# Attention plus top-1 experts in one kernel: the split of the row maxima moved ahead of the pair's accumulating transfer in GpSimd's order

## The chip, the core and the metric

One core of a Trainium2 chip runs the whole program. Its engines are TensorE (PE in the profile; PEld are its weight loads), VectorE (DVE), ScalarE (ACT), GpSimd (POOL) and SyncE (SP), which only issues DMAs here. Each engine works through its own list of instructions in order, and engines wait for one another and for DMAs by semaphores. The core has 16 DMA engines. What SP issues goes to them through one queue (q1 in the profile), what GpSimd issues through another (q0). The metric is the device time of one execution in microseconds (us), less is better; the time of a kernel is the median of several runs.

## What is computed

Four sequences of 2048 tokens with 512 features pass through a layer norm, a multi-head attention and a layer of eight experts with a capacity of 100 tokens each. Both results are added to the input.

```
xn = layernorm(x)                               # x: 4 x 2048 x 512, float32
q, k, v = split(xn @ w_qkv); 16 heads of 32     # q and k filtered by a 32 x 32 matrix
attn = softmax(q @ k.T / sqrt(32))              # 2048 x 2048 for each head and sequence
out = x + (attn @ v) @ w_out + b_out + experts(xn)
```

Most of the work is the attention: 64 pairs of a sequence and a head, each with a 2048 x 2048 table of scores, its exponentials and its product with v.

## The kernel before

**Groups, blocks and windows.** The main loop takes groups k = 0 to 15, each one sequence with four heads (128 features). A group has four blocks n of 512 queries; I number the 64 blocks 0 to 63, so that block 4k + n is the block n of group k. A block has eight windows w of two key tiles j (`even` and `odd`, 128 keys each), 512 windows in all. The inner loop stands at lines 905 to 957.

**One window.** For each of its two key tiles and each half u of the heads, TensorE does three things: `shift` (lines 614 to 622) starts a PSUM bank with minus the row's maximum, by a matmul of ones with the tile `negm`; `max_matmuls` makes scores of a later block, which VectorE reduces to row maxima (`part`); `scores` adds q times k to the bank. ScalarE takes the exponential into the tile `even` or `odd` (128 x 2048 float32, 1 MB). One tile later `products` multiplies the tile with v, and VectorE adds that to `num`.

**The pair and the sums.** The softmax's denominator needs the sum of the exponential tiles. One window after the two tiles were made, `pair` (line 892) lets a DMA that GpSimd issues add `odd` to `even` in place, 1 MB with accumulation. Another window later `add_to` (line 895) lets GpSimd add the tile of the window before, in two instructions. The tile `even` has five buffers and `odd` has three, so a buffer of `odd` comes round after three windows and is free once the pair's transfer has landed.

**The maxima.** The maxima of a block are ready two windows ahead of the block. In its window 6 (counting in the block before the one that needs them) `max_close` (line 489) turns them by a matmul and ScalarE copies them to `row[:, 0]` and `rest`. In window 7 `max_split` (line 501) cuts them into three bfloat16 rows of falling size: four small GpSimd instructions, and three SP DMAs of 4 KB each into `negm`. The first of these DMAs needs ScalarE's copy alone, the second and third need GpSimd's. The first matmul of the next block, in `shift`, reads all three rows.

**The end of a block.** `close_steps` (line 649) is spread over the next ten windows: the sums go through DRAM to be inverted and come back as `factor`; in window 7 GpSimd multiplies `num` and `factor` to `ot` (`divide`, line 684); in the window after it TensorE multiplies `ot` with the output weights (`project`, from `result`, line 688).

**Orders.** Every engine keeps the order of the program (`InOrder`, line 71), SP's DMAs in the main loop too. At the start of a window GpSimd gets, in this order, the pair's transfer, the split (in window 7 alone), and the add; then come the steps of `agenda`, a list by window. Two of these matter here: `load_qkv_weights` (line 395, placed at line 861) issues a load of 768 KB (`wg`) on SP in window 6 of a group's last block, and in some groups `load` of 1 MB of x (`xs`) stands beside it (line 875). Projections of the next group are spread over the windows of a group, but for its last one.

Of the kernel before, what the change touches and what calls it, by code (L numbers as in the profile page):

```python
# [101 lines left out]
def attention_and_top1_experts(ctx: ExitStack, tc: tile.TileContext, a: dict, out: bass.AP):  # L102
# [14 lines left out]
    def bank():  # L117

        return array[:, next(turns), :]
# [36 lines left out]
    def chunk(name):  # L156
        tag, bufs = ("y", 1) if name == "y" else ("xs", None)
        return chunks.tile([P, TQ, DM], F32, tag=tag, name=name, bufs=bufs)

    def probs(odd):  # L160

        name = "odd" if odd else "even"
        return probs_pool.tile([P, 2, 2, QB], F32, tag=name, name=name, bufs=3 if odd else 5)
# [296 lines left out]
    def max_matmuls(item, half):  # L460
        k, n, m, t, u = item
        for h in range(2):
            at = DH * (2 * u + h)
            on.tensor.matmul(
                array[:, half[h], :],
                lhsT=qs[k, n][at : at + DH, t * P : (t + 1) * P],
                rhs=ks[k][at : at + DH, m * QB : (m + 1) * QB],
                start=True,
                stop=True,
            )  # L470

    def max_reduce(item, half):
        k, n, m, t, u = item
        if (k, n) not in parts:
            parts[k, n] = small.tile([P, HG, TQ, NQ], F32, name="part", bufs=2)
        for heads, scored in joined(*half):
            part = parts[k, n][:, 2 * u : 2 * u + 2, t, m]
            on.vector.reduce_max(part[:, heads], scored, axis=AX.X)
        if (m, t, u) == (NQ - 1, TQ - 1, 0):
            full_blocks.append((k, n))  # L480
# [3 lines left out]
    def max_negate(k, n):  # L484
        negs[k, n] = small.tile([P, HG * TQ], F32, name="neg")
        part = parts.pop((k, n)).rearrange("p h t m -> p (h t) m")
        on.vector.tensor_reduce(negs[k, n], part, AX.X, ALU.max, negate=True)

    def max_close(k, n):

        pn = bank()[0 : HG * TQ, 0:P]
        on.tensor.matmul(pn, lhsT=negs.pop((k, n)), rhs=ident, start=True, stop=True)
        rest = small.tile([HG * TQ, P], F32, name="rest")
        row = small.tile([HG * TQ, 3, P], BF16, name="row", bufs=2)
        on.scalar.copy(row[:, 0, :], pn)
        on.scalar.copy(rest, pn)
        closed[k, n] = rest, row
# [3 lines left out]
    def max_split(k, n):  # L501

        rest, row = closed.pop((k, n))
        for i in (1, 2):
            on.gpsimd.tensor_tensor(rest, rest, row[:, i - 1, :], ALU.subtract)
            on.gpsimd.tensor_copy(row[:, i, :], rest)
        negms[k, n] = qkv.tile([P, QB], BF16, tag="negm", name="negm", bufs=3)
        for i in range(3):
            on.sync.dma_start(out=negms[k, n][i::DH, :], in_=row[:, i, :])
# [93 lines left out]
    def scores(k, n, j, u, half):  # L603
        for h in range(2):
            at = DH * (2 * u + h)
            on.tensor.matmul(
                half[h],
                lhsT=ks[k][at : at + DH, j * P : (j + 1) * P],
                rhs=qs[k, n][at : at + DH, :],
                start=False,  # L610
                stop=True,
            )

    def shift(k, n, u, half):
        for h in range(2):
            at = DH * (2 * u + h)
            on.tensor.matmul(
                half[h],
                lhsT=ones_b[at : at + 3, :],
                rhs=negms[k, n][at : at + 3, :],  # L620
                start=True,
                stop=False,
            )
# [6 lines left out]
    def products(k, n, j, tile, num):  # L630
        po = bank()
        four_heads(po, lambda at: vs[k][:, j, at], tile, start=True, stop=True)
        if j == 0:
            on.scalar.copy(num, po)
        else:
            on.vector.tensor_tensor(num, num, po, ALU.add)
# [172 lines left out]
    def at(window, step, *args):  # L809
        agenda[window].append(lambda: step(*args))  # L810
# [81 lines left out]
    def pair(first, second):  # L892
        on.gpsimd.dma_start(out=first, in_=second, accum_op=ALU.add)

    def add_to(tile, sum_before, engine):
        for u in range(2):
            engine.tensor_tensor(tile[:, u], tile[:, u], sum_before[:, u], ALU.add)

    pairs, adds, full, splits = {}, {}, {}, {}
    left = None  # L900
    window = 0
    maxima = stream[MAX_AHEAD:]
    for k in range(B * NG):
        plan(k)
        for n in range(NQ):
            num = work.tile([P, QB], F32, tag="num", name="num")
            tiles = {}
            for w in range(NW):
                even, odd = w * WIN, w * WIN + 1
                if window in pairs:  # L910
                    pair(*pairs.pop(window))
                if window in splits:
                    max_split(*splits.pop(window))
                if window in adds:
                    add_to(*adds.pop(window))
                here = agenda[window]
                cut = (len(here) + 1) // 2
                for j in (even, odd):
                    tiles[j] = probs(j == odd)
                    for u in range(2):  # L920
                        half = bank(), bank()

                        mate = maxima.pop(0) if maxima else None
                        shift(k, n, u, half)
                        if mate:
                            mh = next(turns), next(turns)
                            max_matmuls(mate, mh)
                        scores(k, n, j, u, half)
                        for h in range(2):
                            on.scalar.activation(tiles[j][:, u, h, :], half[h], AF.Exp, scale=SCALE)  # L930
                        if mate:
                            max_reduce(mate, mh)
                    while full_blocks:
                        filled = full_blocks.pop(0)
                        max_negate(*filled)
                        full[window + 1] = filled
                    if left:
                        products(*left)
                    left = k, n, j, tiles[j], num
                    if j == even and window in full:  # L940
                        splits[window + 1] = full.pop(window)
                        max_close(*splits[window + 1])
                    for step in here[:cut] if j == even else here[cut:]:
                        step()
                last = (k, n) == (B * NG - 1, NQ - 1)
                if not last or w < NW - 2:
                    pairs[window + 1] = tiles[even], tiles[odd]
                    if 0 < w:

                        due, engine = (2, on.gpsimd) if maxima else (3, on.vector)  # L950
                        adds[window + due] = tiles[even], tiles[even - WIN], engine
                if last and w == NW - 2:
                    y = chunk("xs")
                    on.sync.dma_start(out=y, in_=o[B - 1, n])
                window += 1
            if not last:
                for after, *step in close_steps(k, n, num, tiles[NT - WIN]):
                    at(window + after, *step)
# [41 lines left out]
```

## Time and profile before

| what | value |
|---|---|
| time, median of 3 runs (lowest to highest) | 4525.47 us (4524.64 to 4526.17) |
| the profiled execution: time, span | 4519.14 us, 4517.2 us |
| TensorE busy | 4390.0 us, 97% of the span |
| GpSimd busy | 2919.2 us, 65% |
| VectorE busy, ScalarE busy | 3134.8 us, 2596.8 us |
| granted TensorE clock, mean | 0.987 |
| q0, the transfers that GpSimd issues | 605.83 MB, 68.9% of the 16 DMA engines' span |
| q1, the transfers that SP issues | 93.89 MB, 6.7% |
| pair's transfers | 510 of 1024 KB, landing a median of 8.1 us after the issue |
| GpSimd's TENSOR_TENSOR on `rest`, CAST to `row` | 128 each, 417 ns and 287 ns |
| GpSimd's `even` adds | 876, 2517 ns each |

The span runs from the first instruction to the last. Busy time of TensorE is from records in which a matmul's end is modelled, so a share of 97% says that it is nearly always at work, not that it is at its peak. A row of the waits names the engine and the tile that waited, what it waited for, the sum in us, the number of times and the longest. A row of the timeline gives a start, a length, the instruction, how many of them were merged, and in brackets how long the engine had been idle before it and for what. A row of the stretches (windows of the profile, not of the kernel) gives a stretch, its length, the busy time of each engine, then the granted TensorE clock, the busy share of the DMA engines (it can pass 1 in a short stretch, since a packet counts where it starts) and the GB/s moved.

### The profile page before, as it was taken

Reading aid. Unit: us, or ns where it says so; the run is one execution under the profiler, and the core shown is the slowest. Engines: PE = TensorE matmul, PEld = TensorE weight load, DVE = VectorE, ACT = ScalarE, POOL = GpSimd, SP = SyncE. Lnnn points to the kernel's source line nnn. Section 1 sums busy time; section 2 is a strip of 40 time slices with the busy share of each in tenths; the row PEclk is TensorE's granted clock in tenths of the full one; section 3 lists DMA queues with packets and bytes.
Section 4 is the critical chain, followed back from the end, with each engine's and each line's share of the span. In section 5 each row is a group of like instructions: output and inputs, shape, how many; then the busy total and the mean of one; then the engine's idle time right before and its main releaser. Section 6 shows DMA issues by size and latency. Waiting matters only on the chain. (4 is left out here: it accounts for less than half of the span.)

```text
span 4517.2 us, 106256 instructions
## 1 busy us (share of the span) xinstructions
PE 4390.0 (97%) x44398; PEld 1883.0 (42%) x44398; DVE 3134.8 (69%) x3642; ACT 2596.8 (57%) x4988; POOL 2919.2 (65%) x1993
## 2 busy tenths in 40 slices
PE   8999999999999999999999999999999999999998
PEld 4343433434434343444444434343443434434432
DVE  6667667766676777776666766677667765777776
ACT  3455555575555555557555555556655555555555
POOL 0677666765766666775676656667567665776673
PEclk9999999999999999999999999999999999999999
DMA  4677778886777777897677777789767866787778
GB/s 107 157 165 156 152 144 163 196 196 129 144 153 149 145 156 152 167 215 168 131 147 149 159 140 142 156 177 208 160 130 159 167 141 127 149 169 157 149 157 176
DMA packets 191546, 707.03 MB, mean 157 GB/s; under 512 B 47374, under 2 KB 52656, under 8 KB 125784
## 3 DMA queue, kind: packets, MB, share of 16 engines
q0 software_dynamic: 110432, 605.83, 68.9%
q1 hardware_dynamic: 79456, 93.89, 6.7%
q8 instruction: 347, 5.69, 0.5%
q14 instruction: 135, 1.11, 0.1%
q10 hardware_dynamic: 1176, 0.52, 0.0%
HBM read 76.03 MB, written 89.98 MB: 37 GB/s over the span
## 5 line engine op out<-in xcount | busy, mean ns | idle before, releaser
L82 DVE TENSOR_REDUCE part<-array 128x2 f32<-128x1024 f32 (+1 forms) x2313 | 2434.8, 1097 | 1251.7 <-PE array L82 1239.6
L82 PE MATMUL array<-k,q 32*128 32x512 f32 x8192 | 2242.4, 626 | 4.6 <-issue 2.2
L82 POOL TENSOR_TENSOR even<-even 128x1024 f32<-128x1024 f32 x876 | 2118.2, 2517 | 183.0 <-DMA even<-odd 181.8
L82 PE MATMUL array<-q,k 32*128 32x512 f32 x8192 | 2068.7, 598 | 0.8 <-issue 0.8
L82 ACT ACTIVATE even<-array 128x512 f32<-128x512 f32 x2048 | 1066.3, 601 | 540.9 <-PE array L82 536.7
L82 ACT ACTIVATE odd<-array 128x512 f32<-128x512 f32 x2048 | 1060.1, 602 | 429.0 <-issue 221.4
L82 POOL DMA_DIRECT2D even<-odd x510 | 442.0, 867 | 1227.6 <-ACT odd L82 1032.7
L82 PEld LDWEIGHTS array<-k,q 32*128 32x128 f32 x8192 | 811.3, 185 | 165.6 <-DVE num L82 68.4
L82 PE MATMUL array<-negm,ones_b 3*128 3x512 bf16 x4096 | 799.1, 384 | 78.7 <-DMA negm<-row 70.5
L82 PEld LDWEIGHTS array<-q,k 32*128 32x128 f32 x8192 | 755.3, 187 | 16.5 <-issue 6.8
L82 DVE TENSOR_TENSOR num<-num,array 128x512 f32<-128x512 f32 x960 | 651.2, 678 | 50.5 <-PE array L82 31.2
L82 PEld LDWEIGHTS <-ones_b 3*128 3x128 bf16 x4096 | 203.4, 92 | 968.7 <-issue 805.5
L82 PE MATMUL array<-even,v 128*32 128x512 f32 x4096 | 549.6, 607 | 14.4 <-ACT odd L82 14.4
L82 PE MATMUL array<-odd,v 128*32 128x512 f32 x4096 | 555.3, 613 | 4.7 <-ACT even L82 4.5
L82 PE MATMUL array<-xnT,wg 128*32 128x512 f32 x4096 | 465.5, 595 | 1.3 <-ACT xnT L82 0.7
L82 PE MATMUL array<-wo,ot 128*32 128x512 f32 x2048 | 259.3, 596 | 1.7 <-POOL ot L82 1.7
L82 PEld LDWEIGHTS array<-xnT,wg 128*32 128x32 f32 x4096 | 132.7, 111 | 307.2 <-issue 271.1
L82 PEld LDWEIGHTS array<-odd,v 128*32 128x32 f32 x4096 | 81.9, 109 | 405.6 <-ACT even L82 397.2
L82 PEld LDWEIGHTS array<-even,v 128*32 128x32 f32 x4096 | 81.1, 108 | 406.4 <-ACT odd L82 393.5
L82 PEld LDWEIGHTS array<-wg,xnT 128*32 128x32 f32 x8192 | 226.2, 110 | 41.4 <-issue 23.8
L82 PE MATMUL array<-wg,xnT 128*32 128x128 f32 x8192 | 235.7, 273 | 1.9 <-issue 1.9
L82 ACT COPY y<-array 128x512 f32<-128x512 f32 x252 | 147.7, 586 | 138.3 <-PE array L82 137.7
(127 smaller groups left out, 1354.5 us busy)
## 6 DMA issues: line engine op xcount, KB each, us to landing
even<-odd POOLq DMA_DIRECT2D x510, 1024.0 KB, 8.1
out_dram<-y POOLq DMA_DIRECT2D x63, 1024.0 KB, 12.1
xs<-in_L_attn_x_dram SPq DMA_DIRECT2D x30, 1024.0 KB
out_dram<-xs SPq DMA_DIRECT2D x16, 1024.0 KB
factor<-inverse SPq DMA_DIRECT2D x248, 64.0 KB
wg<-wd SPq DMA_DIRECT2D x15, 768.0 KB
wo<-in_L_attn_w_out_dram SPq DMA_DIRECT2D x16, 256.0 KB
negm<-row SPq DMA_DIRECT2D x192, 4.0 KB
```

Of the source, the lines that this page charges most:

```text
L82: done = act(*args, **kwargs)
```

## The change

In the inner loop the call of `max_split` moves from behind `pair` to ahead of it. Nothing else is altered: the same instructions and DMAs run, with the same tiles and buffers.

```
@@ -907,10 +907,10 @@
             for w in range(NW):
                 even, odd = w * WIN, w * WIN + 1
+                if window in splits:
+                    max_split(*splits.pop(window))
                 if window in pairs:
                     pair(*pairs.pop(window))
-                if window in splits:
-                    max_split(*splits.pop(window))
                 if window in adds:
                     add_to(*adds.pop(window))
                 here = agenda[window]
```

```
def max_split(k, n):
    rest, row = closed.pop((k, n))
    for i in (1, 2):
        on.gpsimd.tensor_tensor(rest, rest, row[:, i - 1, :], ALU.subtract)
        on.gpsimd.tensor_copy(row[:, i, :], rest)
    negms[k, n] = qkv.tile([P, QB], BF16, tag="negm", name="negm", bufs=3)
    for i in range(3):
        on.sync.dma_start(out=negms[k, n][i::DH, :], in_=row[:, i, :])

def pair(first, second):
    on.gpsimd.dma_start(out=first, in_=second, accum_op=ALU.add)
```

It touches 63 of the windows: window 7 of every block but the last, ahead of blocks 1 to 63. The split of block 0 stands ahead of the main loop and stays. On GpSimd the split's four instructions come ahead of the pair's issue. Among SP's instructions nothing changes places, since the pair's transfer is issued by GpSimd.

## The prediction

> **What bounds the kernel now.** TensorE is busy for 97% of the span, so I read the waits first, for what stops it.
>
> ```profile
> POOL even L82 <- ACT odd L82: 1032.7, 307, 12.1
> ...
> PE array L82 <- DMA negm<-row: 70.5, 22, 7.0
> ```
>
> TensorE's longest sum of idle time is 70.5 us, in 22 waits for the rows of the maxima. GpSimd waits 1032.7 us for ScalarE's `odd` tile, which is what the pair's issue needs, and the split is queued behind that issue. The timeline of GpSimd, SP and TensorE ahead of block 60 shows how the 22 come about:
>
> ```profile
> 4251.36 4.68 POOL L82 TENSOR_TENSOR even<-even 128x1024 f32<-128x1024 f32 x2 [1.46 <-DMA even<-odd]
> 4255.97 0.85 POOL L82 DMA_DIRECT2D even<-odd  x1
> 4256.57 0.42 POOL L82 TENSOR_TENSOR rest<-rest,row 16x128 f32<-16x128 f32 x1
> ...
> 4257.89 0.28 POOL L82 CAST row<-rest 16x128 bf16<-16x128 f32 x1
> 4258.14 4.65 POOL L82 TENSOR_TENSOR even<-even 128x1024 f32<-128x1024 f32 x2
> 4262.76 1.25 POOL L82 TENSOR_TENSOR ot<-num,factor 128x512 f32<-128x512 f32 x1
> ```
>
> ```profile
> 4257.35 0.54 SPq L82 DMA_DIRECT2D negm<-row  x1
> ...
> 4258.19 1.03 SPq L82 DMA_DIRECT2D negm<-row  x1
> ```
>
> ```profile
> 4263.77 0.61 PE L82 MATMUL array<-negm,ones_b 3*128 3x512 bf16 x2 [4.13 <-DMA negm<-row]
> ```
>
> The split begins 0.60 after the pair's issue and lasts 1.60 us (4256.57 to 4258.17); SP issues the last row 0.03 later. That row has 4 KB, but TensorE gets it only 5.6 us later. The stretches of the same time (length, five engines, granted clock, DMA share, GB/s) say why:
>
> ```profile
> 4256.50:4257.50 1.00, 1.00 (x12) 0.63 (x13) 0.95 (x2) 0.20 (x1) 0.85 (x4) 1.00 0.56 115
> ...
> 4261.50:4262.50 1.00, 0.00 (x0) 0.00 (x0) 0.00 (x0) 0.00 (x0) 1.00 (x1) 1.00 0.69 134
> 4262.50:4263.50 1.00, 0.00 (x0) 0.00 (x0) 0.00 (x0) 0.00 (x0) 1.00 (x2) 0.52 0.05 13
> 4263.50:4264.50 1.00, 0.73 (x6) 0.76 (x10) 0.00 (x0) 0.00 (x0) 1.00 (x2) 0.50 0.00 0
> 4264.50:4269.00 4.50, 4.50 (x26) 1.69 (x23) 2.39 (x2) 2.07 (x4) 4.50 (x3) 0.50 0.94 189
> ```
>
> The pair's megabyte moves until about 4262.2; the packet records have the rows' packets at 4262.4 to 4262.6, behind all of it. And TensorE's clock, which fell to half in the stall, stays there till 4269.
>
> **A rule against this change.** The Trainium skill ("DMA: Bandwidth & Descriptors", section on queues, rings and completion order) says that a DMA engine takes turns between its queues packet by packet. Then the pair would hardly hold back 4 KB, and the change would give only the earlier start: in the 22 places the split would begin 22 us earlier in sum (0.60 each, and 8.8 us of pair waits), so at most 22 us. The row decides: in block 60 the rows waited out a whole transfer.
>
> **The race to the queue.** In the new order the split begins when GpSimd's add and ScalarE's copy to `rest` are both over. In block 60 that is 4256.0 (the copy was done at 4250.6). It ends at 4257.6; the last row is issued at 4257.65, the pair at 4257.6. Who reaches the DMA engines first? Ahead of block 9 a row was issued on idle queues at 715.77, and stretches of 0.1 us show its packets from here:
>
> ```profile
> 716.80:716.90 0.10, 0.10 (x5) 0.07 (x1) 0.10 (x1) 0.10 (x1) 0.00 (x0) 1.00 0.00 0
> 716.90:717.00 0.10, 0.10 (x6) 0.00 (x0) 0.10 (x1) 0.10 (x1) 0.00 (x0) 1.00 0.10 23
> ```
>
> That is 1.18 us after its issue; its semaphore was complete at 717.4, after 1.65. The pair's issue at 4255.97 has its first large packet 1.43 later. So the last row is at the engines at 4258.83 and the pair at 4259.03: the row wins by 0.2 us and lands at 4259.3. TensorE is free for it at 4259.64 (4263.77 less 4.13). The stall is gone.
>
> **The stalls, block by block.** I did the same for all 22: new start, 1.60, 1.65, against the time at which TensorE came.
> - In 17 the row lands in time: 46.7 us.
> - Ahead of blocks 12, 28 and 36 SP has the `wg` load (in the first two also 1 MB of `xs`) in its queue ahead of the rows. There the first row, which the change doesn't touch, landed only at 931.0, 2031.4 and 2589.1, and the others can only follow it. Of 3.54, 3.60 and 4.64 us some 3.1, 3.1 and 2.5 stay: 3.0 us saved.
> - Ahead of blocks 61 and 63 GpSimd's add ends too late: of 4.97 and 7.04 some 1.0 and 3.1 stay: 7.9 us saved.
>
> Sum 57.6 us.
>
> **The clock.** After 16 of the stalls the q and k matmuls take 1.06 instead of 0.59 us for 2.3 to 4.2 us, 63.0 us together; half of that is lost, 31.5. It stays in blocks 12, 28, 36 and 63 (7.5), so 24.0 are saved. A check: the first windows of blocks 4, 32 and 48, after stalls too short for it, take 11.43 us; those of 8, 16, 20, 24, 36, 40 and 56 take 15.2 us more in sum, where half of their slow stretches is 13.5. The skill's page "TensorE: Matmul & The Clock Gate" (Part 1) has the half clock after an idle window of about 3.4 us. By that, ten stalls cost 1.7 each, and 10 us would be saved. But the records show half clock after stalls of 2.27, 2.35 and 2.52 us too; I take 24.0.
>
> **What is late next: `ot`.** In the window after the stall TensorE reads `ot` 3.02 us after its first matmul. GpSimd's `ot` doesn't come earlier where the pair's issue followed the add without a gap (split and issue only change places), and up to 1.6 us earlier elsewhere. TensorE now gets there first ahead of ten blocks (4, 16, 24, 32, 44, 48, 56, 60, 61, 62), by 0.8, 0.8, 0.3, 0.7, 0.6, 0.8, 3.4, 1.5, 1.7 and 0.8: a new wait of 11.4 us, and some 1.6 of half clock after the longest. Cost 13.0.
>
> **What I put at nothing.** The split's 1.60 us now stand ahead of the pair's issue. In some 40 of the 63 windows GpSimd had a gap there and it costs the transfer little; in the others the transfer starts up to 1.6 us later. Queued behind it are an add one window on, and `odd`'s buffer two windows on, some 11 us after the issue even in group 15, against 7 to 8 for the transfer. GpSimd idles 1227.6 us before 510 pair issues, 2.4 us a window, which takes up the add. Without that cover it would be at most 63 x 1.6 = 101 us; below nothing it can't be. SP's instructions keep their order; what is queued behind the rows is issued sooner. The split's new wait for ScalarE's copy is over before GpSimd comes, or ends ahead of the pair's own.
>
> **Sum.** 57.6 + 24.0 - 13.0 = 68.6 us. The profiled execution would go from 4519.14 (span 4517.2) to 4450.5. The median of the runs is 6.3 above that one; I take the same 68.6 off 4525.47: **4457 us**, 1.5% faster.
>
> **The rivals.**
> - *The race is lost (slower).* The last row has 0.2 us in hand. If it reaches the engines behind the pair's first packets, it waits out the transfer as before, and that starts later: by 1.6 us in 13 of the 22 places (no gap ahead of the issue) and by 5.5 us together in the other nine. That is 26 us more, 4552. For it: what decides is a fifth of a microsecond between two issue paths that no row shows side by side. Against it: both delays scatter by 0.05 only. It decides from 0.2 us of extra delay on SP.
> - *The weight load is what counts.* 14 of the 22 stalls (42.4 us) stand where `wg` was issued just ahead. If rows behind it always wait for a pair too, only the other eight gain: 28.1 less 4.1 that stay, and 7.6 of clock less 4 of new waits, so 28 us, 4497. For it: ahead of block 24 the first row landed at 1754.7, and the second, already issued, at 1759.5. Against it: in 11 of the 14 the first row landed early enough.
> - *Nothing is late behind it.* All 70.5 and 31.5 go: 4423. Against it: `ot` of block 56 ends 6.3 us after TensorE is free.
> - *No effect*, if the rows' landing is set by something that neither order moves.
>
> **How the numbers follow.** A measurement of this kernel can tell about 0.2% (9 us) from no change. Forecast 0.50, weight load 0.15, nothing behind 0.15, no effect 0.05, race lost 0.12, another loss through later transfers 0.03. So faster 0.80, same 0.05, slower 0.15. The range leaves out the last three, 0.20, and takes in the first three with some room: 4420 to 4508. The forecast's own range is 4435 to 4480.
>
> **What would show it.** TensorE's wait for `negm` falls from 70.5 to about 13 us, in some five places; a new row has it waiting about 11 us for `ot`; the stretches behind the group starts have a clock of 1.00, and its mean rises above 0.99. In the split's windows the rows land some 1.7 us after their issue. I am wrong if the 22 waits stay (race lost), if they stay only at the group starts (weight load), or if GpSimd's wait for the pair's landing (191.5 us) grows and TensorE waits for `even`.

## The result, and the profile after

The changed kernel takes 4446.9 us (median of 4 runs, 4441.7 to 4452.6) against 4525.06 us (4 runs, 4524.6 to 4526.2): a ratio of 0.983, with an interval of 0.981 to 0.984. It is 78 us faster; 69 were forecast. The profiled executions stand at 4452.56 and 4519.14, spans of 4449.2 and 4517.2, so their difference is 67 to 68 us: the profiled one is the slowest of the four after. The mean granted clock went from 0.987 to 0.994.

The waits of the kernel after, in us, times and the longest:

```profile
POOL even L82 <- ACT odd L82: 876.5, 259, 10.5
...
PE array L82 <- POOL ot L82: 20.3, 13, 3.4
...
PE array L82 <- DVE part L82: 9.2, 7, 5.1
...
PE array L82 <- DMA negm<-row: 3.9, 2, 3.0
```

TensorE's wait for the rows has gone from 70.5 us in 22 places to 3.9 in two (blocks 61 and 63). Its wait for `ot` has come up from 1.7 to 20.3 us. Rows to go with these, first two views of before (waits, then busy times), then the same two of after:

```profile
POOL even L82 <- DMA even<-odd: 191.5, 141, 6.9
...
PE array L82 <- DVE part L82: 4.3, 5, 1.9
...
PE array L82 <- POOL ot L82: 1.7, 1, 1.7
```

```profile
PE 4390.0 (97%) x44398; PEld 1883.0 (42%) x44398; DVE 3134.8 (69%) x3642; ACT 2596.8 (57%) x4988; POOL 2919.2 (65%) x1993
```

```profile
POOL even L82 <- DMA even<-odd: 234.7, 166, 7.0
```

```profile
PE 4365.1 (98%) x44398; PEld 1869.4 (42%) x44398; DVE 3132.2 (70%) x3642; ACT 2595.9 (58%) x4988; POOL 2943.6 (66%) x1993
```

GpSimd waits 156 us less for `odd`; the split, 1.6 us ahead of 63 pairs, can fill at most 101 of them. Its wait for the pair's landing grew by 43 us. That is one half of a sign of being wrong that the prediction named; the other half, TensorE waiting for `even`, did not come (4.5 us in 9 places before and after). The timeline of GpSimd, SP and TensorE ahead of block 60, to be laid beside the one of before:

```profile
4192.80 4.67 POOL L82 TENSOR_TENSOR even<-even 128x1024 f32<-128x1024 f32 x2 [1.50 <-DMA even<-odd]
4197.44 0.42 POOL L82 TENSOR_TENSOR rest<-rest,row 16x128 f32<-16x128 f32 x1
...
4198.77 0.28 POOL L82 CAST row<-rest 16x128 bf16<-16x128 f32 x1
4199.26 0.88 POOL L82 DMA_DIRECT2D even<-odd  x1 [0.21 <-issue]
...
4204.50 1.57 POOL L82 TENSOR_TENSOR ot<-num,factor 128x512 f32<-128x512 f32 x1
```

```profile
4199.07 0.53 SPq L82 DMA_DIRECT2D negm<-row  x1
```

```profile
4201.40 0.39 PE L82 MATMUL array<-negm,ones_b 3*128 3x512 bf16 x2
...
4206.12 1.06 PE L82 MATMUL array<-wo,ot 128*32 128x512 f32 x8 [1.46 <-POOL ot L82]
```

The split follows the add at once. The last row is issued at 4199.07, its semaphore is complete at 4200.7, and the first matmul of the block starts without a gap. The read of `ot` behind it waits 1.46 us, where 1.5 were forecast. Stretches of 0.1 us show the race that the forecast hung on:

```profile
4200.20:4200.30 0.10, 0.10 (x4) 0.00 (x0) 0.10 (x1) 0.10 (x1) 0.10 (x1) 1.00 0.11 26
4200.30:4200.40 0.10, 0.10 (x4) 0.00 (x1) 0.10 (x1) 0.10 (x1) 0.10 (x1) 1.00 0.09 15
4200.40:4200.50 0.10, 0.10 (x7) 0.10 (x8) 0.10 (x1) 0.10 (x1) 0.10 (x1) 1.00 0.00 0
...
4200.70:4200.80 0.10, 0.10 (x4) 0.00 (x0) 0.10 (x1) 0.10 (x1) 0.10 (x1) 1.00 4.42 901
```

The little traffic from 4200.2 to 4200.4 is the last row, the burst at 4200.7 the pair's megabyte. The row's last packet starts a third of a microsecond ahead of the pair's first.

### The profile page after: what moved, and what is told of

Its sections match the earlier page's. It is cut to its first block, busy times and chain, and to the rows that moved or that the text cites. A ratio compares the mean times of both kernels' runs of the same rounds, so it can differ in the third digit from the quotient of the medians.

```text
span 4449.2 us, 106256 instructions
## 1 busy us (share of the span) xinstructions
PE 4365.1 (98%) x44398; PEld 1869.4 (42%) x44398; DVE 3132.2 (70%) x3642; ACT 2595.9 (58%) x4988; POOL 2943.6 (66%) x1993
## 5 line engine op out<-in xcount | busy, mean ns | idle before, releaser
L82 PE MATMUL array<-k,q 32*128 32x512 f32 x8192 | 2220.1, 621 | 2.6 <-DVE part L82 1.9
L82 PE MATMUL array<-q,k 32*128 32x512 f32 x8192 | 2046.9, 593 | 0.7 <-issue 0.7
L82 POOL DMA_DIRECT2D even<-odd x510 | 458.6, 899 | 1105.7 <-ACT odd L82 876.5
L82 PE MATMUL array<-wo,ot 128*32 128x512 f32 x2048 | 261.8, 601 | 20.3 <-POOL ot L82 20.3
```

The costliest lines, as they stand in the source:

```text
L82: done = act(*args, **kwargs)
```

## The experiments

Two explanations fit this result. Either the rows must be at the DMA engines ahead of the pair's transfer (theory A), or it helps that GpSimd starts the split sooner (rival B, which is what turns between the queues would give). The third, rival C, was that the rows stand behind the load of `wg`. Each run below is compared with runs of the kernel before on the same chip.

**e1: no earlier start, but ahead of the pair.** GpSimd reads a little of `odd` ahead of the split, so the split can't start before the pair could.

```
+def await_odd(tile):
+    seen = small.tile([P, 2, 2, 1], F32, name="seen")
+    on.gpsimd.tensor_copy(seen, tile[:, :, :, 0:1])
...
 if window in splits:
+    await_odd(pairs[window][1])
     max_split(*splits.pop(window))
```

> The changed order, but GpSimd first reads one column of each quarter of the pair's odd tile, so that the split can't start before ScalarE has finished odd, as in the kernel before; the split still stands ahead of the pair's transfer. Theory A (the rows must reach the DMA engines ahead of the pair's transfer): the rows land about 1.7 us after their issue, TensorE's wait for negm stays under 8 us, and the time within 8 us of the changed kernel's, so 4440 to 4456. Rival B (what counts is that GpSimd starts the split sooner): the rows are issued at most 0.5 us sooner than in the kernel before, so at most 11 us are gained on it: above 4510, with a wait for negm above 55 us.

Measured: 4447.06 us, ratio 0.982 (0.981 to 0.984), and this row of its waits:

```profile
PE array L82 <- DMA negm<-row: 9.5, 4, 4.7
```

The wait is a little above the 8 us named, with 4.7 of it ahead of block 44; the time is that of the changed kernel. The whole gain is there with the earlier start taken away. B falls. The rows need not even be issued first: ahead of block 9 SP issues the last row at 710.02, 0.07 us behind the pair (709.95), and by the packet records (the trace's list of single DMA packets) its packets still start first, at 711.18 to 711.28 against 711.40 for the pair's. What counts is who is first at the DMA engines.

**e2: the earlier start, but one cast behind the pair.** The split starts as in the changed kernel; only its last instruction, 0.3 us long, stands behind the pair's issue.

```
 on.gpsimd.tensor_tensor(rest, rest, row[:, i - 1, :], ALU.subtract)
+if i == 2 and between:
+    pair(*between)
 on.gpsimd.tensor_copy(row[:, i, :], rest)
...
-max_split(*splits.pop(window))
+max_split(*splits.pop(window), pairs.pop(window))
```

> The changed order, but the fourth of the split's instructions (the cast of the third row) stands behind the pair's transfer; the split starts as soon as in the changed kernel and the third row is issued about 1 us sooner after the pair than in the kernel before. Theory A: the third row's packets meet the transfer, it lands as the transfer ends, and TensorE's 22 waits for negm come back, longer by up to 1.2 us in the 13 places without a gap: a wait of 65 to 90 us and a time of 4520 to 4550, not faster than before. Rival B: the third row is 0.3 us later than in the changed kernel and lands well in time: 4440 to 4460.

Measured: 4526.55 us, ratio 1.0004 (0.9995 to 1.0013). From its waits, and from its timeline ahead of block 60, SP, GpSimd and TensorE:

```profile
PE array L82 <- DMA negm<-row: 69.8, 20, 8.7
```

```profile
4255.88 0.89 POOL L82 DMA_DIRECT2D even<-odd  x1
4256.47 0.34 POOL L82 CAST row<-rest 16x128 bf16<-16x128 f32 x1
```

```profile
4256.83 0.53 SPq L82 DMA_DIRECT2D negm<-row  x1
```

```profile
4263.64 0.61 PE L82 MATMUL array<-negm,ones_b 3*128 3x512 bf16 x2 [5.33 <-DMA negm<-row]
```

The last row is issued 0.95 us behind the pair instead of 0.2 ahead of it, and TensorE gets it 6.8 us after its issue. One of three rows behind the pair costs the whole gain. This is the "race is lost" case of the prediction; it came out at no change instead of 26 us of loss. The wait and the time lie in the ranges given for theory A.

**e3: the weight load out of the way, the order as before.** The load of `wg` is placed one window later, behind the split's DMAs on SP.

```
-at(start + GW - 2, load_qkv_weights, k + 2)
+at(start + GW - 1, load_qkv_weights, k + 2)
```

> The kernel before (pair ahead of the split) with the 768 KB load of wg one window later, so that SP issues it behind the rows. Theory A: the rows still meet the pair's transfer and the wait for negm stays at 60 to 75 us; the time stays at 4525 or rises by TensorE's waits for wg. Rival C (rows stand behind the weight load): the 14 stalls at the group starts, 42 us, go, and the wait for negm falls below 32 us.

Measured: 4497.04 us, ratio 0.994 (0.992 to 0.996).

```profile
PE array L82 <- DMA negm<-row: 49.2, 21, 4.9
```

Neither expectation holds. The waits don't go, 21 are left, so it isn't the place behind `wg` in SP's queue that makes them. But they are shorter at ten of the 14 group starts: ahead of block 36 the last row landed 10.1 us after the pair's issue before and 7.6 here. By the packet records the load had held back the start of the pair's transfer, and the rows with it: the pair's first packet came 4.2 us after its issue before and 1.4 here, while the transfer itself took 5.7 us before and 6.0 here. That was no part of either theory.

**e4: what is late next.** The division to `ot` goes ahead of the add in GpSimd's order, on top of the change.

```
 if window in pairs:
     pair(*pairs.pop(window))
+if window in divides:
+    divides.pop(window)()
 if window in adds:
...
+if step[0].__name__ == "divide":
+    divides[window + after] = step[0]
+else:
     at(window + after, *step)
```

> The changed kernel with GpSimd's multiplication to ot ahead of the add in its window instead of behind it. If ot is what is late next (theory A's second half): ot is ready 4.7 us sooner, TensorE's wait for ot falls from 20.3 us to about 2 (the 1.7 us at the end of the kernel stay), the half-clock stretches behind it go (some 5 us), and the time falls by 15 to 25 us to 4422 to 4432. If the waits for ot only hide another wait: the time stays within 6 us of the changed kernel's and the waits turn up at another tile.

Measured: 4433.49 us, ratio 0.980 (0.978 to 0.982). TensorE's wait for `ot` is 1.7 us again, and GpSimd waits 18.0 us for `factor`:

```profile
POOL ot L82 <- DMA factor<-inverse: 18.0, 15, 2.5
```

So `ot` was what is late next. The gain over the changed kernel is 13 us in the medians, just short of the 15 expected: 10.0 us of waits for the rows were left in this profile, more than in the one of the changed kernel.

**e5 to e8: towards a better kernel.** In the profile after, the 5.1 us wait for `part` comes from a second transfer of this kind: `few`, 8 KB from SP, issued at 4295.42 while a pair's transfer was moving (its packets run from 4293.0 to 4298.4), with VectorE's inversion waiting for it. e5 puts the inversion one window later on top of e4, e6 the weight load of e3 on top of e4, e7 both; e8 is the changed kernel again beside them.

```
-steps = [(2, fold), (3, fetch), (4, invert), (5, spread), (7, divide)]
+steps = [(2, fold), (3, fetch), (5, invert), (5, spread), (7, divide)]
```

> As e4 (split first, division ahead of the add), with VectorE's inversion of the sums one window later, so that it no longer waits for a small SP transfer that stands behind a pair's. Theory A, seen at a second place (few behind the pair): the wait of VectorE for few and the one stall of 5.4 us behind it in group 15 go, with its half clock: 5 to 9 us under e4, 4424 to 4430. If factor then comes too late, GpSimd waits for it longer than the 18 us of e4 and TensorE's wait for ot returns: 4435 or more.

> As e4, with the weight load one window later as in e3. In e3 that shortened the stalls at the group starts because the load took part of the pair's transfer rate; with the split ahead of the pair only the rests should be left, 5.8 us of the wait for negm in e4 (blocks 28 and 40): 4424 to 4434, wait for negm under 5 us. If the load instead meets the projections' start, a wait for wg shows and the time rises over 4440.

> Split first, division ahead of the add, inversion one window later and weight load one window later. If the parts are independent: 4418 to 4428.

> The changed kernel itself, on the same chip as the three above: 4440 to 4453 as in its own runs.

| run | median us | ratio to before, 95% interval |
|---|---|---|
| e5, inversion later | 4519.12 | 0.998 (0.997 to 0.999) |
| e6, weight load later | 4428.72 | 0.978 (0.977 to 0.979) |
| e7, both | 4490.44 | 0.992 (0.990 to 0.993) |
| e8, the changed kernel | 4451.88 | 0.982 (0.981 to 0.984) |

e6 beats both kernels. Its wait for the rows is 3.0 us, in one place; its interval overlaps that of e4, so the 5 us between their medians are not shown to be a gain, but it lies clear of that of e8, which ran beside it. e5 was a plain miss. Its waits, and GpSimd and SP ahead of block 4:

```profile
POOL ot L82 <- DMA factor<-inverse: 93.9, 31, 9.3
...
PE array L82 <- DMA negm<-row: 71.6, 15, 8.8
```

```profile
382.56 0.90 POOL L82 DMA_DIRECT2D even<-odd  x1 [0.22 <-ACT even L82]
```

```profile
383.06 0.37 SPq L82 DMA_DIRECT2D wg<-wd  x1
383.47 2.90 SPq L82 DMA_DIRECT2D negm<-row  x3
```

The split is in time and ahead of the pair, but SP isn't: it works in order, and the four DMAs of `factor` waited for an inverse that came a window later. All three rows are issued behind the pair's transfer and the load, and ahead of seven group starts (blocks 4, 12, 16, 28, 32, 44 and 48) the stalls are back at 6.7 to 8.8 us each. The race can be lost on SP's side as well as on GpSimd's. e7 missed its 4418 to 4428 in the same way, with a smaller loss (56.7 us of waits for the rows).

## Why the prediction was right

- *The mechanism.* Rows that are at the DMA engines ahead of the pair's transfer land some 1.6 us after their issue, rows behind it wait it out: e1 and e2 show it from both sides. By the packet records the rows' last packet starts 3.5 to 7.9 us after the last row's issue in the 63 windows of the kernel before, and 4.6 to 9.0 in those of e2. After the change it is 1.3 to 1.4 us in 49 of them; in the other 14, all ahead of a group's first or second block, it is 1.7 to 4.6.
- *The rule set aside.* The rule of turns by packet, which the prediction set aside for a row of the trace, would have given at most 22 us as the prediction read it. That reading left something out: the same section of the Trainium skill ("DMA: Bandwidth & Descriptors", "Queues, rings and completion order") puts a turn at some 9 to 17 descriptors. The packet records have each pair's megabyte as 128 packets of 8 KB, an estimated 8 for each of the 16 engines, so one turn could be the whole transfer. That fits block 60, where no packet of the rows starts between the pair's 128. It doesn't fit ahead of block 12 in the same trace: there 68 packets of 8 KB on q0 and 64 of 2 KB on q1 start between 921 and 924 us, and on most engines, as far as the times of the packets tell them apart, they alternate one by one. In block 12 SP's queue was moving data when the pair came; in block 60 it was not. Whether that decides was not tried. So that the rows wait out the pair is shown; why they get no turn stays open.
- *The race.* A lead of 0.2 us, from first packet to first packet, was forecast from two separate rows; block 60 shows 0.47 (4200.24 and 4200.71). GpSimd's issue of the pair came 0.21 us after the last cast, which the sum hadn't. In e1, where the row has no such help (issued 0.07 us behind the pair), the lead is 0.2 (711.18 and 711.40). Two readings of the prediction were a little off: ahead of block 60 of the kernel before the rows' packets start until 4262.8, not 4262.6, and the row ahead of block 9 was complete 1.6 us after its issue, not 1.65.
- *The stalls.* 57.6 us were to go, 66.6 went in the profiled execution (70.5 less 3.9). Blocks 61 and 63 kept 0.95 and 2.96, as worked out (1.0 and 3.1). Blocks 12, 28 and 36, for which 8.7 us were kept, lost all of it. There the step was that the first row, which the change doesn't touch, lands when it did before. It didn't: ahead of block 36 it landed 7.6 us after its issue before and 4.4 after. The pair is now issued 2.64 us behind the weight load instead of 0.55, so the rows, which stand behind the load on SP, meet only the pair's first packets. It isn't settled for good: e8 waited 2.5 and 4.7 us ahead of blocks 28 and 44, and this scatter fits the spread of the changed kernel's runs, though no run shows that it makes it.
- *The clock.* TensorE's busy time fell by 24.9 us (4390.0 to 4365.1), for which 24.0 less 1.6 were put down. That all of it is clock is not shown, but the same instructions ran.
- *What is late next.* 11.4 us of wait for `ot` were forecast, 18.6 came (20.3 less 1.7). The term was mis-sized where the stalls were: ahead of blocks 12, 28 and 44 `ot` costs 1.3, 2.2 and 2.0 us, for which 0, 0 and 0.6 stood, as TensorE now comes sooner; that is 4.8 of the 7.2 us. The longest, ahead of block 56, is 3.36 us against 3.4.
- *The sum.* TensorE's idle time fell by 43.1 us and its busy time by 24.9, together the 68.0 by which the span shrank; 68.6 were forecast. That this is so close is partly luck: 9.0 us too few were put down for the stalls, 2.5 too few for the clock, 7.2 too few for the cost of `ot`, and nothing for TensorE's wait for `part`, which rose by 4.9 (4.3 to 9.2). These errors nearly cancel. The medians differ by 78, since the profiled executions lie at other places among their runs.
- *The rivals.* "Race lost" was priced 26 us too high, going by e2: the pair's later start made single stalls longer (8.65 us ahead of block 63) and others shorter, 69.8 in sum. But e2 delays the pair by less than the 1.6 us of that sum. "Weight load" named a real part, not the cause.

## What to carry to other kernels

A few KB that an engine is waiting for shouldn't be issued behind a megabyte on another queue: here 0.95 us behind it cost all of 80 us; 0.2 ahead was enough, and so was 0.07 behind (e1), as SP's packets started sooner after their issue than GpSimd's (ahead of block 9, 1.16 us against 1.45). Look at the order of issue across queues, not only inside one, and at what else the small transfer's own queue waits for (e5). When a stall goes, the next one can be read off beforehand from the ends of the other engines' work against the time at which the freed engine will arrive.

## What the runs showed of the hardware

- Ahead of block 60 of the kernel before, the 4 KB rows on q1 were moved only at 4262.4 to 4262.8, after the pair's megabyte on q0, whose last packets start at 4261.9. It isn't so clean where SP's loads run too: ahead of block 12 the rows' packets came scattered over the transfer.
- A lead over one pair doesn't help behind another: the 8 KB of `few` were issued 0.6 us ahead of a pair in e4 (4274.20 against 4274.79), and VectorE still waited 6.5 us for them. The pair issued at 4266.99 was moving then; its packets run from 4274.0 to 4279.6, and those of `few` start at 4278.3.
- TensorE's clock fell to half after stalls of 2.27 (block 16), 2.35 (block 13), 2.52 (block 52) and 2.73 us (block 44), not only after the longer ones, and stayed there for 3.4 us, after block 52's for 6.8.
